# Key, query and output products of three cross-attention layers, each as two 64-column products, and the denominators scheduled one step later

## The chip, the core and the metric

The kernel runs on one core of a Trainium2 chip. The metric is the time of one execution on the device, in microseconds (us); lower is better. The engines of the core are named as the profile names them: PE (matrix products; PEld is its weight loading), DVE, ACT and POOL (element-wise work), SP (it issues nearly all DMA transfers here).

## The reference

Four cross-attention layers follow each other on x (2048 rows of 256 values), all with the same context of 1601 rows of 512 values. Layers 0, 2 and 3 are the **masked** ones: 16 heads of 64 values, and a bias on the logits of four token columns.

```python
q = x @ Wq                      # 256 -> 1024 = 16 heads x 64
k = ctx @ Wk; v = ctx @ Wv      # 512 -> 1024
logits = einsum('bhqd,bhkd->bhqk', q, k) * 64**-0.5 + col_bias   # col_bias: mask by token column
probs = softmax(logits, axis=-1)
out = einsum('bhqk,bhkd->bhqd', probs, v)
x = out.reshape(...) @ Wo + bo + x
```

Layer 1 is the **grouped** one: RMS norm of x, 16 query heads of 16 values over 4 key/value heads, softmax, output product, residual. Everything is float32.

## The kernel before

**Tiling.** A masked layer is done in 8 blocks of two heads (2 x 64 = 128 feature columns); a block has four units, one for each 512 query rows. The 1601 keys are 13 chunks (twelve of 128, one of 65), and a unit takes 13 steps, one per chunk, two steps at a time ("pair of steps"). The grouped layer has 4 blocks of four heads in a scheme of its own.

**A step of a masked unit.** `masked_scores` (L715) makes the transposed scores of both heads, 128 keys x 512 queries each, from two products with 64 contracted rows. ACT copies them out (L727) into one of 22 buffers `p`, and DVE keeps a running maximum (L732). When a unit's 13 steps are through, `maxima` transposes the maxima on PE (L775), DVE reduces them (L776), and two DMAs by way of DRAM (`cols`, then `spread`, L678 and L681) put them on all partitions; ACT copies that to PSUM (L801). 18 steps after its scores a chunk gets the subtraction (DVE, L806), the exponential (ACT, L811) and its share of the sum (POOL, L814 for the first chunk, L816 for the others), and two steps later the product with the values (PE, L851): two products of 128 contracted rows and 64 columns, one for each head, the first into partitions 0 to 63 of `po`, the second into 64 to 127.

**The pieces.** Between these steps PE gets "pieces" of other work:

- keys of the next block (`keys`, L461): for two chunks at a time, 128 weight columns, four products of 128 rows in a row, over 256 columns of context; the 13th chunk is alone, with 65 columns;
- values of the next block (`two_values`, L415): 128 context columns as weights, 128 columns of Wv moving;
- queries of the next unit (`queries`, L485): 128 weight columns, two products over 512 columns;
- the finish of a unit: `add_up` (L884) sums the denominators over partitions, in two products of 64 columns; ACT copies the result to `by` (L888), two small DMAs bring it to `dens` (L893); `denominators` takes the reciprocal (DVE, L901), sends it to DRAM (`cols`, L678) and fetches it back to all partitions of `by` (two DMAs, L681); `divide` multiplies on POOL (L920); `project` makes the output product (L930), 128 weight columns, two products over 512 columns, and adds to x (L937, L942).

**What sets the order.** PE, DVE and ACT keep the written order, held by dependencies without semaphores at the end of the function; POOL and SP keep theirs as queues. `finish` gives each piece of a masked unit's end a due step, counted from the step in which the unit's last values are made; `Pieces.own` takes what is due up to the later step of a pair. So a due step of +2 lies in the next pair in any case, and one of +3 in the next pair for a unit that ends in the first step of a pair, and one pair later for a unit that ends in the second. 13 is odd, so units of the two kinds alternate. Pieces due come first; keys and values of the next block fill up, at most one piece that shares `pm` to a pair; after a unit's last scores the pieces come ahead of the next scores. A unit of the last block of layers 0 and 2 has `at = 10`, other masked units `at = 12`; the last block of layer 3 has a list of its own.

**Tiling of a product.** PE can hold products of fewer rows or columns beside each other. The built program names for each product which division of the array it uses: the scores (L715) 64 rows x 128 columns, the values (L851) and `add_up` (L884) 128 x 64, and keys, values' projection, queries, output product and transposes the whole 128 x 128. A float32 product is two passes in the trace, so the four products of two steps' values show as x8.

Of the kernel before, what the change touches and what calls it, by code (L numbers as in the profile page):

```python
# [18 lines left out]
P = 128  # L19
# [7 lines left out]
Piece = namedtuple("Piece", "run cost shared", defaults=(True,))  # L27
# [7 lines left out]
def tile_cross_attention_stack(ctx: ExitStack, tc: tile.TileContext, t: dict, out: bass.AP):  # L35
# [33 lines left out]
    nc = tc.nc  # L69
# [5 lines left out]
    NCT = CT // P  # L75
# [179 lines left out]
    def width(c):  # L255

        return sum(m for _, m in TCH[c : c + 2])
# [146 lines left out]

    factors = dram.tile([NB, P, QT], FP, name="factors")

    def two_values(v, wv, c, ct):

        f = wv.shape[2]
        chunks = TCH[c : c + 2]  # L410
        m = chunks[0][1]
        pv = ps_m.tile([P, QB // P, P], FP, name="pm")
        for d, (_, md) in enumerate(chunks):
            for k in range(NCT):
                nc.tensor.matmul(  # L415
                    pv[:md, d, :f], ct(k)[:, d * P : d * P + md], wv[:, k, :],
                    start=(k == 0), stop=(k == NCT - 1),
                )
        nc.scalar.copy(v[:m, c : c + len(chunks), :], pv[:m, : len(chunks), :f])  # L419
# [5 lines left out]
    class Masked:  # L425
# [26 lines left out]
        def projections(self, u):  # L452


            def keys(c, ct):
                if u.kT is None:
                    u.kT = heads.tile([P, T], FP, name="kT")
                a, n = TCH[c][0], width(c)
                pk = ps_m.tile([P, QB], FP, name="pm")[:, :n]
                for k in range(NCT):  # L460
                    nc.tensor.matmul(pk, u.wk[:, k, :], ct(k), start=(k == 0), stop=(k == NCT - 1))  # L461
                nc.scalar.copy(u.kT[:, a : a + n], pk)

            def values(c, ct):
                if u.v is None:
                    u.v = heads.tile([P, NT, P], FP, name="v")
                two_values(u.v, u.wv, c, ct)

            return keys, values
# [7 lines left out]
        def query_pieces(self, unit):  # L477

            xt = unit.transposed_x()

            def queries():
                unit.q = heads.tile([P, QB], FP, name="q", bufs=3)
                pq = ps_m.tile([P, QB], FP, name="pm")
                for k in range(NC):
                    nc.tensor.matmul(  # L485
                        pq, unit.u.wq[:, k, :], xt[:, k, :], start=(k == 0), stop=(k == NC - 1)
                    )
                nc.scalar.mul(unit.q, pq, 64 ** -0.5)

            return [(11, Piece(queries, 2.0))]  # L490

    class Grouped:
# [44 lines left out]
        def projections(self, u):  # L537

            if u.n:
                return None  # L540

            def keys(c, ct):
                if self.ks is None:
                    self.ks = heads.tile([64, T], FP, name="ks", bufs=1)
                a, n = TCH[c][0], width(c)
                pk = ps_m.tile([P, QB], FP, name="pm")[:64, :n]
                for k in range(NCT):
                    nc.tensor.matmul(
                        pk, self.wk[:, k, :], ct(k), start=(k == 0), stop=(k == NCT - 1)
                    )  # L550
                nc.scalar.copy(self.ks[:, a : a + n], pk)

            def values(c, ct):
                if self.vs is None:
                    self.vs = heads.tile([P, NT, 64], FP, name="vs", bufs=1)
                two_values(self.vs, self.wv, c, ct)

            return keys, values
# [125 lines left out]
    class Unit:  # L684
# [239 lines left out]
        def project(self):  # L924

            k = 0
            for py in psum.heads(False)[0]:
                of = range(k, k + py.shape[1])
                for k in of:
                    nc.tensor.matmul(  # L930
                        py[:, k - of[0], :], self.u.wo[:, ts(k, P)], self.oT, start=True, stop=True
                    )
                k += 1
                if self.masked and self.u.n == self.layer.BLOCKS - 1 - (self.l == len(layers) - 1):
                    for j in of:
                        bo, to = bo_of[self.layer.l][:, j : j + 1], xs[:, self.b, j, :]
                        nc.vector.scalar_tensor_tensor(  # L937
                            to, py[:, j - of[0], :], bo, to, ALU.add, ALU.add
                        )
                else:  # L940
                    to = xs[:, self.b, of[0] : k, :]
                    nc.vector.tensor_tensor(to, py, to, ALU.add)  # L942
# [41 lines left out]
        def finish(self):  # L984

            if self.very_last:
                return [(0, Piece(lambda: self.quarters(of[len(units) - 2]), 2.0))]
            if self.final:

                at = 4 if self.b == NB - 2 else 2  # L990
                found = [
                    (at, Piece(self.add_up, 1.0)), (at + 2, Piece(self.denominators, 0.0)),
                    (at + 4, Piece(self.divide, 0.0)),
                ]
                if self.b < NB - 2:
                    found.append((10 - 2 * self.b, Piece(self.project_rows, 2.0, False)))
                return found
            if not self.masked:
                return [
                    (1, Piece(self.den_columns, 0.0)), (3, Piece(self.denominators, 0.0)),  # L1000
                    (6, Piece(self.divide, 0.0)), (8, Piece(self.project, 2.0, False)),
                ]

            at = 10 if self.u.n == self.layer.BLOCKS - 1 else 12
            return [
                (2, Piece(self.add_up, 1.0)), (4, Piece(self.denominators, 0.0)),
                (at - 4, Piece(self.divide, 0.0)), (at, Piece(self.project, 2.0, False)),
            ]

# [5 lines left out]
    for b in range(NB):  # L1015
        nc.scalar.dma_start(
            out=x_rows[b], in_=x[0, ts(b, QB), :].rearrange("(n p) c -> p n c", p=P)
# [377 lines left out]
```

## Time and profile before

| | |
|---|---|
| median of 3 runs | 4650.75 us (4649.49 to 4656.12) |
| the profiled execution | 4649.11 us, its span 4647.2 us |
| PE busy | 4529.5 us (97% of the span) |
| DVE, ACT, POOL busy | 3611.4, 3263.8, 2983.5 us (78%, 70%, 64%) |
| mean granted PE clock | 0.987 |
| products in the program | 12,524, in two passes each where they are float32 |

The span is the time from the first to the last instruction on the core. The busy time of an engine is the union of its instructions; for PE the ends of products are modelled, so the distances between the starts of consecutive groups say more than the busy share. In a timeline row the first number is the start in us from the span's start, the second how long the group lasted, and `x8` the number of passes in it.

### The profile page before, as it was taken

What the parts mean: (1) busy time and instruction counts of PE and PEld (TensorE: products, weight loads), DVE (VectorE), ACT (ScalarE), POOL (GpSimd) and SP (SyncE); (2) the same over time, 40 slices, a digit from 0 to 9 for tenths busy, and PEclk for the clock granted to TensorE, in tenths of its full rate; (3) what the DMA queues carried; (4) which work ended last, traced back from release to release, by engine and by line L of the source; (5) the groups of instructions that cost most, each with busy time, mean ns of one, the idle gap of its engine ahead of it and who ended that gap; (6) DMA issues with size and microseconds to landing.
All of it is one profiled execution on the core that took longest, in us unless ns stands there. A gap on an engine that the chain in (4) does not pass through costs nothing.

```text
span 4647.2 us, 64011 instructions
## 1 busy us (share of the span) xinstructions
PE 4529.5 (97%) x23563; PEld 1853.4 (40%) x23563; DVE 3611.4 (78%) x3672; ACT 3263.8 (70%) x4108; POOL 2983.5 (64%) x1436
## 2 busy tenths in 40 slices
PE   8999999999899999999999999999999999999998
PEld 5444434443333333343344444344444444344432
DVE  5888888888766666652678888888888888888887
ACT  5777777777645555555667777777777777777776
POOL 3888888888620000000578887888888888878887
PEclk9999999999989999998899999999999999999999
DMA  5333333233201100021233333233232323332311
GB/s 160 85 90 82 87 81 88 78 86 84 71 24 34 28 22 22 20 62 31 70 91 82 88 82 87 77 88 85 77 94 82 92 82 87 81 88 78 85 38 39
DMA packets 377252, 338.01 MB, mean 73 GB/s; under 512 B 143781, under 2 KB 332741, under 8 KB 376940
## 3 DMA queue, kind: packets, MB, share of 16 engines
q1 hardware_dynamic: 373670, 328.54, 26.2%
q8 instruction: 186, 3.05, 0.3%
q0 software_dynamic: 1152, 3.28, 0.2%
q10 hardware_dynamic: 2118, 2.10, 0.1%
q14 instruction: 126, 1.03, 0.1%
HBM read 318.49 MB, written 14.69 MB: 72 GB/s over the span
## 4 chain that ended last, share of the span: by engine, by line
PE 90%; DVE 4%; ACT 2%; POOL 1%; issue 1%; DMA 1%; SPq 0%; ACTq 0%; DVEq 0%; POOLq 0%
PE po L851 28%; PE s L715 23%; PE t L746 9%; PE pm L415 6%; PE pm L461 6%; PE pm L485 4%; PE s L930 4%; DVE top L732 3%; PE s L775 2%; PE pm L884 2%; ACT p L727 2%; POOL sums L816 1%; PE t L821 1%; PE s L821 1%; PE pm L597 1%
## 5 line engine op out<-in xcount | busy, mean ns | idle before, releaser
L816 POOL TENSOR_TENSOR sums<-sums,p 128x1024 f32<-128x1024 f32 x1145 | 2714.9, 2371 | 627.3 <-ACT p L811 555.1
L732 DVE TENSOR_TENSOR top<-s,top 128x1024 f32<-128x1024 f32 (+1 forms) x1056 | 1290.8, 1222 | 344.6 <-ACT p L727 288.8
L851 PE MATMUL po<-p,v 128*64 128x512 f32 (+3 forms) x8320 | 1500.9, 526 | 6.4 <-ACT p L811 3.7
L806 DVE TENSOR_TENSOR p<-p,b 128x1024 f32<-128x1024 f32 (+1 forms) x1248 | 1478.2, 1208 | 1.9 <-ACT b L801 1.7
L727 ACT COPY p<-s 128x1024 f32<-128x1024 f32 (+1 forms) x1248 | 1224.0, 1015 | 336.2 <-PE s L715 276.8
L715 PE MATMUL s<-q,kT 64*128 64x512 f32 (+1 forms) x4992 | 1295.9, 625 | 43.8 <-DVE top L732 39.8
L811 ACT ACTIVATE p<-p 128x1024 f32<-128x1024 f32 (+1 forms) x1248 | 1264.6, 1058 | 39.5 <-DVE p L806 39.1
L851 PEld LDWEIGHTS po<-p,v 128*64 128x64 f32 (+3 forms) x8320 | 367.2, 125 | 1128.3 <-issue 989.1
L715 PEld LDWEIGHTS s<-q,kT 64*128 64x128 f32 (+1 forms) x4992 | 403.9, 182 | 756.3 <-DVE top L732 383.2
L833 ACT ACTIVATE p<-t 128x512 f32<-128x512 f32 (+1 forms) x760 | 413.9, 594 | 296.8 <-PE t L821 256.4
L759 DVE TENSOR_REDUCE row_top<-t 128x1 f32<-128x512 f32 x700 | 451.3, 687 | 199.1 <-PE t L821 166.5
L920 POOL TENSOR_TENSOR by<-oT,by 128x512 f32<-128x512 f32 x111 | 141.1, 1271 | 708.5 <-DMA by<-cols 521.6
L821 PE MATMUL t<-q,kT 32*128 32x512 f32 (+1 forms) x1520 | 489.6, 644 | 0.0
L746 PE MATMUL t<-kT,q 32*128 32x512 f32 (+1 forms) x1880 | 482.7, 553 | 0.0
L415 PEld LDWEIGHTS pm<-wv,ct 128*128 128x128 f32 (+1 forms) x2600 | 302.4, 187 | 89.2 <-issue 67.1
L415 PE MATMUL pm<-wv,ct 128*128 128x128 f32 (+2 forms) x2600 | 326.9, 278 | 2.2 <-ACT v L419 0.9
L461 PE MATMUL pm<-ct,wk 128*128 128x256 f32 (+1 forms) x1344 | 309.2, 373 | 3.6 <-DMA ct<-ctxT 2.1
L461 PEld LDWEIGHTS pm<-ct,wk 128*128 128x128 f32 x1344 | 233.3, 191 | 119.1 <-issue 83.2
L730 DVE TENSOR_TENSOR top<-s,p 128x1024 f32<-128x1024 f32 x96 | 117.6, 1225 | 202.8 <-ACT p L727 202.7
L746 PEld LDWEIGHTS t<-kT,q 32*128 32x128 f32 x1880 | 182.8, 185 | 164.1 <-issue 97.4
L776 DVE TENSOR_REDUCE ntop<-s 128x8 f32<-128x1024 f32 x96 | 117.6, 1225 | 123.7 <-PE s L775 123.7
L930 PE MATMUL s<-by,wo 128*128 128x512 f32 x376 | 187.8, 622 | 12.6 <-issue 6.9
(173 smaller groups left out, 2085.8 us busy)
## 6 DMA issues: line engine op xcount, KB each, us to landing
ct<-ctxT SPq DMA_DIRECT2D x288, 512.0 KB
xT<-xT SPq DMA_DIRECT2D x100, 512.0 KB
spread<-cols SPq DMA_DIRECT2D x96, 512.0 KB
by<-cols SPq DMA_DIRECT2D x190, 128.0 KB
xT<-xs SPq DMA_DIRECT2D x16, 512.0 KB
ct<-ctxT SPq DMA_DIRECT2D x48, 130.0 KB
wk<-in_L_xattn_Wk_dram SPq DMA_DIRECT2D x24, 256.0 KB
wv<-in_L_xattn_Wv_dram SPq DMA_DIRECT2D x24, 256.0 KB
```

Source lines behind the costliest of these rows:

```text
L415: nc.tensor.matmul(pv[:md, d, :f], ct(k)[:, d * P : d * P + md], wv[:, k, :], start=(k == 0), stop=(k == NCT - 1),)
L461: nc.tensor.matmul(pk, u.wk[:, k, :], ct(k), start=(k == 0), stop=(k == NCT - 1))
L715: nc.tensor.matmul(s[:m, h, :], self.u.kT[r, a : a + m], self.q[r, :], start=True, stop=(a != TAIL),)
L727: nc.scalar.copy(p[:m], s[:m])
L732: nc.vector.tensor_tensor(self.top[:m], s[:m], self.top[:m], ALU.max)
L746: nc.tensor.matmul(s[:, at : at + n], self.q[r, ts(q, P)], self.u.kT[r, a : a + n], start=True, stop=True,)
L759: nc.vector.tensor_reduce(self.top[:, of, q, k : k + 1], s, AX.X, ALU.max)
L806: nc.vector.tensor_tensor(self.p[c][:m], self.p[c][:m], self.less[:m], ALU.add)
L811: nc.scalar.activation(p[:m], p[:m], AF.Exp)
L816: nc.gpsimd.tensor_tensor(self.sums[:m], self.sums[:m], p[:m], ALU.add)
L821: nc.tensor.matmul(s[:m], self.u.kT[r, a : a + m], self.q[r, :], start=True, stop=True)
L851: nc.tensor.matmul(to, v, p, start=(c == 0 and not part), stop=(c == NT - 1 and part != 0))
```

## The change

`halved` makes a product with 128 weight columns as two products of 64 columns, into partitions 0 to 63 and 64 to 127 of the same output, in the order in which the values' products of the two heads come. Keys, queries and the output product of the masked layers use it; the values' projection, the transposes and the grouped layer stay as they were. In the finish of a masked unit the due steps of `add_up` and `denominators` become `at - 9` and `at - 7`: 3 and 5 instead of 2 and 4 where `at` is 12, and 1 and 3 in the last block of layers 0 and 2, where it is 10. `divide` and `project` keep their due steps. Lines after the new function move down by 7.

```diff
+    def halved(out, cols, rows, **kwargs):
+        n = cols.shape[-1]
+        step = 64 if n == P else n
+        for at in range(0, n, step):
+            nc.tensor.matmul(out[at : at + step], cols[:, at : at + step], rows, **kwargs)
...
                 for k in range(NCT):
-                    nc.tensor.matmul(pk, u.wk[:, k, :], ct(k), start=(k == 0), stop=(k == NCT - 1))
+                    halved(pk, u.wk[:, k, :], ct(k), start=(k == 0), stop=(k == NCT - 1))
...
                 for k in range(NC):
-                    nc.tensor.matmul(
+                    halved(
                         pq, unit.u.wq[:, k, :], xt[:, k, :], start=(k == 0), stop=(k == NC - 1)
                     )
...
                 for k in of:
-                    nc.tensor.matmul(
+                    (halved if self.masked else nc.tensor.matmul)(
                         py[:, k - of[0], :], self.u.wo[:, ts(k, P)], self.oT, start=True, stop=True
                     )
...
             at = 10 if self.u.n == self.layer.BLOCKS - 1 else 12
             return [
-                (2, Piece(self.add_up, 1.0)), (4, Piece(self.denominators, 0.0)),
+                (at - 9, Piece(self.add_up, 1.0)), (at - 7, Piece(self.denominators, 0.0)),
                 (at - 4, Piece(self.divide, 0.0)), (at, Piece(self.project, 2.0, False)),
             ]
```

## The prediction, made before the changed kernel ran

> **What bounds the kernel.** I read the page first, then the masked stretch by itself, then PE's timeline there.
>
> ```profile
> span 4647.2 us, 64011 instructions
> PE 4529.5 (97%) x23563; PEld 1853.4 (40%) x23563; DVE 3611.4 (78%) x3672; ACT 3263.8 (70%) x4108; POOL 2983.5 (64%) x1436
> PE 90%; DVE 4%; ACT 2%; POOL 1%; issue 1%; DMA 1%; SPq 0%; ACTq 0%; DVEq 0%; POOLq 0%
> ```
>
> PE is busy all along, and 90% of the chain that ended last is PE's. The stretch from 2400 to 4400 us holds masked layers alone; the first line gives its busy times, the second is the longest of PE's own waits in it.
>
> ```profile
> 2400.00:4400.00 2000.00, 1975.36 (x8841) 823.07 (x8840) 1681.17 (x1497) 1528.81 (x1785) 1635.20 (x746) 1.00 0.32 85
> PE s L715 <- DVE top L732: 18.9, 50, 0.8
> ```
>
> PE (1975 of 2000) is the bound; DVE (1681), POOL (1635) and ACT (1529) have a sixth or more to spare. A unit takes some 37.5 us, and PE waits about 0.4 us in it. So what the PE stream loses in length is what the time can lose.
>
> What does the stream consist of? The groups' starts in PE's timeline tell. Durations overlap, so I take the distance from one start to the next.
>
> ```profile
> 1005.54 1.94 PE L851 MATMUL po<-p,v 128*64 128x512 f32 x8
> 1007.40 1.98 PE L485 MATMUL pm<-xT,wq 128*128 128x512 f32 x4
> 1009.23 1.11 PE L775 MATMUL s<-ident,top 128*128 128x128 f32 x8
> 1010.18 1.95 PE L415 MATMUL pm<-wv,ct 128*128 128x128 f32 x16
> 1012.06 1.99 PE L715 MATMUL s<-q,kT 64*128 64x512 f32 x8
> ...
> 1019.63 2.05 PE L415 MATMUL pm<-wv,ct 128*128 128x128 f32 x16
> 1021.61 1.99 PE L715 MATMUL s<-q,kT 64*128 64x512 f32 x8
> 1023.53 1.94 PE L851 MATMUL po<-p,v 128*64 128x512 f32 x8
> 1025.39 1.98 PE L930 MATMUL s<-by,wo 128*128 128x512 f32 x4
> 1027.21 1.95 PE L415 MATMUL pm<-wv,ct 128*128 128x128 f32 x16
> 1029.09 1.08 PE L851 MATMUL po<-p,v 65*64 65x512 f32 x4
> ```
>
> And one place where two groups of the tiling 128 x 64 meet (the grouped layer's keys, 64 weight columns, 65 moving columns):
>
> ```profile
> 1150.53 1.94 PE L851 MATMUL po<-p,v 128*64 128x512 f32 x8
> 1152.30 0.63 PE L548 MATMUL pm<-ct,wk 128*64 128x65 f32 x8
> 1152.86 1.13 PE L715 MATMUL s<-q,kT 64*128 64x512 f32 x4
> ```
>
> Three readings. (a) **A change of tiling costs about 0.20 us when it leads into 128 x 128.** L415 behind another 128 x 128 group (1010.18, 1027.21) takes 1.88 us, behind L851 (1019.63) 1.98: 0.10 for a first weight load that nothing hides. And a group that is followed by another tiling is longer by 0.09: L851 takes 1.86 ahead of L485 or L930, and 1.77 ahead of L548 in its own tiling. Where L930 is followed by L415 in the same tiling, its 1.82 holds the first term alone. (b) **Two halves beside each other cost no more than one whole.** L851's 8 passes of 64 columns, two products at a time, take 1.77 us, entry included, for the work that L930's 4 passes of 128 columns do in 1.82. (c) With 65 moving columns a pass is bound by loading its weights: L548 needs 0.56 us for 8 passes with 64 columns of weights. The masked keys' 65-column group with 128 columns of weights, eight passes too (L461, starting at 1002.37; the next group at 1003.40), needs 1.03.
>
> **The change, part by part.**
>
> *Fewer changes of tiling.* Pieces usually stand between L851 (128 x 64) and L715 (64 x 128). A halved piece has L851's tiling, so the change ahead of it goes and the one behind it stays. Not all gain: queries are often followed by the transposes L775, and the output product by L415, and those then pay the entry that the piece paid before. Counted over PE's instruction lists of the two built programs, entries into 128 x 128 go from 433 to 240; all other kinds stay within 2 (128 x 64: 707 to 708, 64 x 128: 638 in both). 193 x 0.20 = **-39 us**.
>
> *The 65-column keys.* There is one such group in each of 24 blocks: 1.03 - 0.56 = 0.47, less some 0.05 of entry that the first term holds already, 24 x 0.42 = **-10 us**. This takes the two halves' weight loads to run beside each other, as (b) shows for 512 columns. From the other side, if they load one after the other, nothing is won here: 0.
>
> *More instructions.* 672 key, 192 query and 184 output products are doubled: 1048 more. By (b) they cost 0, taking the halves as L851's. One thing no row shows: L851's two halves stream different columns of `p`, the new ones stream the same rows twice. Bounds: 0, or the whole of the pieces once more if the array can't do this side by side. That is 576 key products of 0.43 us (two passes of 256 columns, half of L485's passes), 96 of 0.23, 376 of 0.86: 593 us. I take 0, the nearest row.
>
> The Trainium skill speaks against this part: TensorEngine Tiling (Array Packing), section Performance Considerations (Instruction Overhead), gives each matmul about 60 cycles of overhead and says not to take the tiling factor from a dimension that is already small; its section on when to tile wants 64 columns or fewer, and here there are 128. By that rule the 1048 products, two passes each, would add 2096 x 60 cycles, at the 2.4 GHz of TensorE: Matmul & The Clock Gate (its table of specs) an estimate of 52 us, and the sum would be near zero. The rows of (b) show no such overhead for a second half.
>
> *Denominators later.* With `at` = 12, only units that end in the second step of a pair move: two units in each of 21 blocks, 42 in all. In such a unit (last values copied at 2936.57) `add_up` stands at 2936.7 now, behind the output product, and moves two pairs on; a piece of values or keys takes its place, so PE's work stays the same. Behind it the reciprocal moves from 2948.35 to behind DVE's subtraction of 2952.01, about 2953.2, into the 0.34 us in which DVE waits ahead of L776: no cost. SP then issues the write of the reciprocals at about 2953.6, passing the fetch of the next x, and the two fetches of `by` behind a context slice, just ahead of `spread`. POOL and SP now:
>
> ```profile
> 2948.57 0.36 SPq L678 DMA_DIRECT2D cols<-rden  x1
> 2951.51 1.35 SPq L681 DMA_DIRECT2D by<-cols  x2
> ...
> 2958.21 0.34 SPq L681 DMA_DIRECT2D spread<-cols  x1
> ```
>
> ```profile
> 2944.46 12.14 POOL L816 TENSOR_TENSOR sums<-sums,p 128x1024 f32<-128x1024 f32 x5
> 2956.57 1.27 POOL L920 TENSOR_TENSOR by<-oT,by 128x512 f32<-128x512 f32 x1
> 2959.72 4.83 POOL L816 TENSOR_TENSOR sums<-sums,p 128x1024 f32<-128x1024 f32 x2 [1.89 <-ACT p L811]
> ```
>
> From the write to the first fetch it takes 3.0 us, from that to a divide that waited 3.6 to 5.7 (mostly 3.8 to 4.9) in the units of the other kind. So `by` is there at 2953.6 + 3.1 + 4.4 = 2961.1, and **POOL, free at 2956.6, waits some 4.5 us in the divide**. Queued behind it are the sums of the next unit: L816 starts at 2962.4 instead of 2959.7, 2.7 us late, and stays late for five chunks. Who waits for those? ACT's copy L727, 22 steps after a chunk's scores, needs the buffer back: after these sums it now starts 3.8, 2.3, 7.3, 5.8 and 6.2 us after the sum's end. So one copy (2966.8) comes 0.4 us late, where PE has an output product and keys to do before the next scores at 2973.1 and those scores' buffer would be free 2.6 us early: 0 on PE. The next `add_up`, at 2980.8, follows sums done at 2972.9: covered too. `spread` is issued when its own write has landed, as now (2958.2); its 512 KB may come up to 1 us later behind the 256 KB of `by`. ACT, which waits 0.39 us for it at 2963.47, then waits longer, under the same two pieces: 0 to 0.4 us on PE, 0 to 17 us over 42 units. I take 0, since the pieces cover it. With `at` = 10 units move one pair forward or not at all: no cost.
>
> **Sum.** -39 - 10 = -49 us of PE's stream. PE waits 24.6 us in the 2000 already, mostly for DVE at the start of a unit; some of a gain just ahead of such a wait is given back. DVE idles before those waits too, so they follow PE; I take 10% off, by choice: **-44 us**. The profiled execution (4649.1) would become 4605; the median shown is 1.6 above it, so 4650.75 - 44 = **4607 us**.
>
> **Rivals.**
>
> *Half is given back (4611 to 4641).* DVE is at 84% over the stretch, but two scores tiles are all that PE has ahead. If DVE's maxima keep their times at each unit's start, only about half of the -49 stays: about -25, 4626 us. For it: 50 waits for DVE, one a unit. Against: DVE is idle shortly before them.
>
> *No change (within 9 us).* The halves cost what is saved, 49 us over 1048 products, some 47 ns each. Against it: (b).
>
> *Slower: the divide's wait grows.* Up to a lag of the sums of 2.3 + 2.6 = 4.9 us nothing reaches PE; I expect 2.7. Past that each us costs 42 us. If the fetch of `by` behind a 512 KB slice lands not 4.4 but 8.5 us after its issue, the lag is 6.8, the loss 42 x 1.9 = 80, and the time 4650.75 - 44 + 80 = 4687 us; it outweighs the gain from about 7.7 us. For it: the divide's wait is new and on a queue that is 82% busy. Against: no divide that waited in this stretch shows more than 5.7.
>
> *Slower: the halves don't run side by side*, +593 less the -39 of the changes: about 5205 us. It would decide at once; the values and `add_up` argue against it.
>
> **How the numbers follow.** Forecast (4595 to 4611) 63%; half given back 22%; no change 6%; slower by the divide 6%; halves in series 3%. The range 4595 to 4638 takes the first two (85%). The bound for a change that a measurement of this kernel can tell is 0.2%, 9 us: faster 0.85, same 0.06, slower 0.09.
>
> **What would show it.** Right: L485's group behind L851 with x8 and 1.81 us to a following L715 (1.91 with both changes of tiling now), L851 ahead of it 1.77; the 65-column keys about 0.56; POOL's divide waiting for `by` in every second unit, 4 to 5 us, and PE's waits no longer than now. Wrong: a halved group of over 2 us, or PE waiting for ACT's copies or DVE where it didn't.

## The result, and the profile after

| | before | after |
|---|---|---|
| median | 4651.29 us, 4 runs (4649.49 to 4656.12) | 4693.76 us, 4 runs (4690.64 to 4697.03) |
| ratio, 95% interval | | 1.0085 [1.0073, 1.0097] |
| span of the profiled execution | 4647.2 us | 4688.8 us |
| products in the program | 12,524 | 13,572 |
| entries into the 128 x 128 tiling | 433 | 240 |

The change makes the kernel **slower by about 40 us**; the forecast was 44 us faster. All halved products have line 412, that of the product in `halved`. The page of the changed kernel, its span, busy times and chain by engine:

```profile
span 4688.8 us, 68217 instructions
PE 4501.4 (96%) x25659; PEld 1780.6 (38%) x25659; DVE 3615.3 (77%) x3672; ACT 3266.3 (70%) x4108; POOL 2982.6 (64%) x1436
PE 76%; DVE 10%; issue 5%; ACT 3%; DMA 2%; POOL 2%; another core or an unknown queue 0%; SPq 0%; ACTq 0%; DVEq 0%; POOLq 0%
```

PE's busy time fell by 28 us, as a saving in its stream would have it, but the span grew. PE's share of the chain went from 90% to 76%, and DVE's from 4% to 10%: the end is no longer set by PE alone. The stretch from 2400 to 4400 us (stretch, its length, then PE, PEld, DVE, ACT and POOL busy, with the number of instructions) says the same; behind the busy times stand the granted clock, the DMA share and GB/s:

```profile
2400.00:4400.00 2000.00, 1938.99 (x9886) 773.97 (x9884) 1658.10 (x1475) 1508.17 (x1759) 1611.84 (x736) 1.00 0.32 84
```

All engines are less busy than before at the same granted clock of 1.00: they wait more, for each other or for transfers. **The halves themselves are as forecast.** From PE's timeline:

```profile
3004.83 1.94 PE L858 MATMUL po<-p,v 128*64 128x512 f32 x8
3006.60 1.89 PE L412 MATMUL pm<-xT,wq 128*64 128x512 f32 x8
3008.41 1.08 PE L722 MATMUL s<-q,kT 64*65 64x512 f32 x4
...
3032.07 0.64 PE L412 MATMUL pm<-ct,wk 128*64 128x65 f32 x16
3032.64 2.31 PE L722 MATMUL s<-q,kT 64*128 64x512 f32 x8
```

From start to start, the values ahead of a halved group take 1.77 us, the halved queries 1.81, the 65-column keys 0.57; the three numbers given were 1.77, 1.81 and about 0.56. So the loss is in the waits. PE's and ACT's waits in the stretch (who waits for whom: us in total, times, longest):

```profile
PE s L412 <- issue: 31.5, 21, 2.0
PE s L722 <- DVE top L739: 18.9, 51, 0.6
```

```profile
ACT b L808 <- DMA spread<-cols: 48.6, 23, 4.1
ACT p L734 <- POOL sums L823: 38.9, 43, 1.4
```

In the kernel before, the same two waits were

```profile
PE s L930 <- issue: 4.3, 6, 1.4
ACT b L801 <- DMA spread<-cols: 10.0, 14, 1.6
```

PE's wait for DVE ahead of the scores is 18.9 us, as before. New is the wait of the output product (`s` at L412): 31.5 us in 21 places instead of 4.3 in 6, and another 6.6 us in 6 places that the profile puts down to POOL's sums (0.7 in one before). ACT's wait for `spread` grew from 10.0 us in 14 places to 48.6 in 23; its wait for POOL's sums came to 0.8 us before. POOL now waits some 196 us in the divide, against about 24.

Where does it come from? Units end at two kinds of places, and only those that end in the second step of a pair moved. Taking the copies of `oT` (one a unit) between units 52 and 92, a unit takes 37.58 us before and 37.99 after; the interval behind a unit that didn't move is 37.80 (38.00 before), behind one that moved 38.18 (37.17). All of the loss lies with the kind that moved. One of them in the timeline of the changed kernel, SP's queue first, then lines picked from POOL, ACT, PE and DVE; a bracket holds the engine's idle time just before and what ended it. The unit's last values were copied at 2956.2:

```profile
2972.72 0.37 SPq L685 DMA_DIRECT2D cols<-rden  x1
2974.12 0.36 SPq L685 DMA_DIRECT2D cols<-ntop  x1
2974.75 0.55 SPq L264 DMA_DIRECT2D ct<-ctxT  x1
2978.68 1.12 SPq L688 DMA_DIRECT2D by<-cols  x2
2979.86 0.58 SPq L688 DMA_DIRECT2D spread<-cols  x1
...
2983.72 1.27 POOL L927 TENSOR_TENSOR by<-oT,by 128x512 f32<-128x512 f32 x1 [7.64 <-DMA spread<-cols]
2984.70 1.02 ACT L808 COPY b<-spread 128x1024 f32<-128x1024 f32 x1 [2.16 <-DMA spread<-cols]
2984.95 12.12 POOL L823 TENSOR_TENSOR sums<-sums,p 128x1024 f32<-128x1024 f32 x5
2986.01 1.94 PE L858 MATMUL po<-p,v 128*64 128x512 f32 x8
2987.34 1.01 ACT L734 COPY p<-s 128x1024 f32<-128x1024 f32 x1 [0.38 <-POOL sums L823]
2988.39 1.23 DVE L739 TENSOR_TENSOR top<-s,top 128x1024 f32<-128x1024 f32 x1 [1.35 <-ACT p L734]
2989.71 1.94 PE L412 MATMUL s<-by,wo 128*64 128x512 f32 x8 [1.76 <-issue]
```

The write of the reciprocals (L685, `rden`) stands 1.4 us ahead of that of the maxima (`ntop`). The fetch of `by` is issued 6.0 us after its write, `spread` behind it, 5.7 us after its own. ACT, which runs in its written order, stands 2.16 us before L808, and 0.38 us more, for POOL's sums, before its copy L734. That copy of the scores out of PSUM comes late, so DVE's maximum over that tile (L739, done at 2989.62) is late, and PE's output product, which needs a scores tile to write to, starts at 2989.71 instead of 2987.78 (1.77 after L858): 1.93 us late. The same place before, where the timeline has

```profile
2963.47 1.02 ACT L801 COPY b<-spread 128x1024 f32<-128x1024 f32 x1 [0.39 <-DMA spread<-cols]
...
2966.59 1.94 PE L851 MATMUL po<-p,v 128*64 128x512 f32 x8
2966.95 2.56 DVE L732 TENSOR_TENSOR top<-s,top 128x1024 f32<-128x1024 f32 x2 [0.38 <-ACT p L727]
2968.46 1.98 PE L930 MATMUL s<-by,wo 128*128 128x512 f32 x4
```

shows how little room there was: the first of the two maxima is done at about 2968.2, and the output product starts at 2968.46. With 0.3 us to spare, the lateness reaches PE almost in full: ACT's wait for `spread` is 1.77 us longer than before and its wait for POOL 0.38, together 2.15, and PE is 1.93 late. So in this unit both the late `spread` and POOL have a part, the first the larger one.

A correction to the description of the kernel: PE, DVE and ACT keep the written order, but POOL and SP do not; the build's scheduler orders their queues and they then run in that order. A due step moves their instructions only by way of what these wait for.

### The profile page after: what moved, and what is told of

Same layout as the page of the kernel before. It is cut to its first block, busy times and chain, and to the rows that moved or that the text cites. A ratio compares the mean times of both kernels' runs of the same rounds, so it can differ in the third digit from the quotient of the medians.

```text
span 4688.8 us, 68217 instructions
## 1 busy us (share of the span) xinstructions
PE 4501.4 (96%) x25659; PEld 1780.6 (38%) x25659; DVE 3615.3 (77%) x3672; ACT 3266.3 (70%) x4108; POOL 2982.6 (64%) x1436
## 4 chain that ended last, share of the span: by engine, by line
PE 76%; DVE 10%; issue 5%; ACT 3%; DMA 2%; POOL 2%; another core or an unknown queue 0%; SPq 0%; ACTq 0%; DVEq 0%; POOLq 0%
PE po L858 23%; PE s L722 19%; PE t L753 9%; PE pm L412 7%; PE pm L422 6%; DVE top L739 6%; PE s L412 3%; DVE p L813 3%; ACT p L734 2%; PE s L782 2%; POOL sums L823 2%; PE pm L891 2%; PE t L828 1%; DMA cols<-rden 1%; PE s L828 1%
## 5 line engine op out<-in xcount | busy, mean ns | idle before, releaser
L739 DVE TENSOR_TENSOR top<-s,top 128x1024 f32<-128x1024 f32 (+1 forms) x1056 | 1290.3, 1222 | 330.3 <-ACT p L734 275.0
L858 PE MATMUL po<-p,v 128*64 128x512 f32 (+3 forms) x8320 | 1497.5, 524 | 9.7 <-ACT p L818 6.7
L734 ACT COPY p<-s 128x1024 f32<-128x1024 f32 (+1 forms) x1248 | 1226.3, 1014 | 373.1 <-PE s L722 256.9
L858 PEld LDWEIGHTS po<-p,v 128*64 128x64 f32 (+3 forms) x8320 | 367.9, 125 | 1127.0 <-issue 919.9
L422 PEld LDWEIGHTS pm<-wv,ct 128*128 128x128 f32 (+1 forms) x2600 | 301.2, 188 | 98.5 <-issue 43.4
L422 PE MATMUL pm<-wv,ct 128*128 128x128 f32 (+2 forms) x2600 | 329.7, 279 | 2.8 <-ACT v L426 1.4
L412 PE MATMUL pm<-ct,wk 128*64 128x256 f32 (+1 forms) x2688 | 296.3, 363 | 7.4 <-issue 7.1
L412 PE MATMUL s<-by,wo 128*64 128x512 f32 x728 | 179.6, 613 | 62.9 <-issue 52.4
L412 PEld LDWEIGHTS pm<-ct,wk 128*64 128x64 f32 x2688 | 182.8, 139 | 146.9 <-issue 70.9
```

Of the source, the lines that this page charges most:

```text
L412: nc.tensor.matmul(out[at : at + step], cols[:, at : at + step], rows, **kwargs)
L422: nc.tensor.matmul(pv[:md, d, :f], ct(k)[:, d * P : d * P + md], wv[:, k, :], start=(k == 0), stop=(k == NCT - 1),)
L734: nc.scalar.copy(p[:m], s[:m])
L739: nc.vector.tensor_tensor(self.top[:m], s[:m], self.top[:m], ALU.max)
L858: nc.tensor.matmul(to, v, p, start=(c == 0 and not part), stop=(c == NT - 1 and part != 0))
```

## The experiments

Twelve runs; each ratio is against the kernel before on the same chip.

| run | median us | ratio, 95% interval |
|---|---|---|
| `halves_only` | 4615.66 | 0.9923 [0.9906, 0.994] |
| `due_only` | 4732.26 | 1.0167 [1.0144, 1.0191] |
| `divide_later` | 4703.09 | 1.0114 [1.0096, 1.0133] |
| `spread_first` | 4688.6 | 1.0082 [1.0064, 1.01] |
| `hop` | 4672.01 | 1.0047 [1.0031, 1.0063] |
| `spread_ahead` | 4661.31 | 1.0016 [1.0006, 1.0027] |
| `write_behind` | 4623.25 | 0.9936 [0.992, 0.9952] |
| `fetch_by_act` | 4765.02 | 1.0249 [1.023, 1.0269] |
| `keys_only` | 4640.07 | 0.9973 [0.9961, 0.9985] |
| `queries_only` | 4642.43 | 0.9978 [0.9969, 0.9988] |
| `output_only` | 4642.9 | 0.9975 [0.9967, 0.9984] |
| `values_too` | 4602.38 | 0.9898 [0.9878, 0.9917] |

**The theories.** A: the halves gain, and the move of the denominators costs more. B, the rival: the doubled products cost, and the move is free. Within A: A1, POOL's longer wait in the divide holds its sums back, and with them ACT's copies; A2, the late `spread` holds ACT.

### Which part loses: `halves_only` and `due_only`

`halves_only` is the change with the old due steps; `due_only` is the kernel before with the new ones.

```diff
-                (at - 9, Piece(self.add_up, 1.0)), (at - 7, Piece(self.denominators, 0.0)),
+                (2, Piece(self.add_up, 1.0)), (4, Piece(self.denominators, 0.0)),
```

> The changed kernel with the due steps of before (add_up 2, denominators 4). Theory A: the halves are what was worked out (entries into 128 x 128 fall from 433 to 241, 65-column keys shorter) and the move of the denominators took it back: 4600 to 4618 us. Theory B: the doubled instructions themselves cost more than they save: 4680 to 4700 us, about the changed kernel's time.

> The kernel before with the new due steps alone, products whole. Its own order removes 40 entries into 128 x 128 and 42 into 128 x 64, about 14 us. Theory A: the move costs about 2 us in each of 42 units, less the 14: 4705 to 4735 us. Theory B: the move is harmless: 4635 to 4650 us.

The halves alone gain 0.77%, about 36 us; the move alone costs 1.67%, 78 us. Both lie in the range of theory A. The sum, 42 us, is close to the 40 of the whole change. Theory B falls: 1048 more products, and the time goes down.

### POOL's wait or the late spread: `divide_later`, `spread_first`, `hop`

`divide_later`, the changed kernel with the divide two steps later:

```diff
-                (at - 4, Piece(self.divide, 0.0)), (at, Piece(self.project, 2.0, False)),
+                (at - 2, Piece(self.divide, 0.0)), (at, Piece(self.project, 2.0, False)),
```

> The changed kernel with the divide of masked units due two steps later (at - 2), output product where it was. If POOL's wait in the divide, and the sums queued behind it that hold ACT's copies back, are the cause (A1): most of the loss goes, 4610 to 4640 us, and ACT's copies wait for POOL no longer. If the late spread that holds ACT is the cause (A2): 4670 to 4695 us, unchanged but for a little.

It tells nothing of the theories. The scheduler put POOL's and SP's queues in the same order as without the edit, and the waits are those of the changed kernel (ACT's for `spread` 46.5 us).

`spread_first`, the changed kernel with the fetches of `by` in a piece of their own, due five steps ahead of the output product, in the moved units:

```diff
+            self.fetch_later = at == 12 and self.b % 2 == 1
+            fetch = [(at - 5, Piece(lambda: self.fetch(), 0.0))] if self.fetch_later else []
+            return fetch + [
```

> The changed kernel, but in the 42 moved units the two fetches of by are issued behind spread instead of ahead of it; the divide stays where it is. A2 (late spread): most of the loss goes, 4610 to 4650 us. A1 (POOL's wait in the divide): the divide waits about 1 us longer, so 4690 to 4730 us, while ACT's waits for spread fall from 49 us to about 10 in the stretch from 2400 to 4400 us.

The edit did not do what was meant: the scheduler still left one fetch of `by` ahead of `spread`, so `spread` came no earlier; but it put the divide two sums later on POOL. POOL's waits in the stretch:

```profile
POOL sums L829 <- ACT p L824: 274.0, 106, 4.0
POOL by L934 <- DMA by<-cols: 35.6, 22, 3.4
```

The divide's waits have fallen from some 196 us to about 62, ACT's copies no longer wait for POOL's sums, ACT's wait for `spread` is 49.3 us, and the time is within 5 us of the changed kernel, inside the intervals. So **A1 falls as the main cause**: with POOL's hold on ACT taken away, nearly the whole loss is still there. A small part may be POOL's: behind a unit of the kind that moved, the interval between units 52 and 92 is 37.93 us here, against 38.18 in the changed kernel and 36.71 in `halves_only`.

`hop` does the opposite. It is `halves_only` with one more copy of 4 KB in DRAM ahead of `spread` in the 42 units, and nothing moved:

```diff
+        if hop:
+            again = dram.tile([4, P, QT], FP, name="again", bufs=4)[:n]
+            nc.sync.dma_start(out=again, in_=rows)
+            rows = again
```

> The halves with the due steps of before, and in the 42 units that the change would move spread gets one more small transfer ahead of it (cols to a copy of cols, 4 KB, and spread is fetched from the copy), so that spread alone comes some 2.5 us later; POOL and the denominators stay as they were. A2 (a late spread is what costs): 42 x 2 to 2.5 us on top of 4616, 4690 to 4725 us. A1 (POOL's wait in the divide is what costs): 4612 to 4630 us.

```profile
ACT b L813 <- DMA spread<-again: 47.6, 22, 3.1
```

ACT's wait in the stretch is that of the changed kernel, POOL's divide waits no longer than before, and against `halves_only` the ratio rises by 0.0124, about 58 us. That is below the 4690 to 4725 that A2 expected and far above the 4612 to 4630 of A1. ACT's copy L808 follows the write of the maxima by 10.4 us in the units of this kind, as in the changed kernel (8.9 in `halves_only`). So a `spread` that reaches ACT as late as in the changed kernel, with nothing else moved, costs three quarters of the move's price. The interval behind a unit of this kind is 37.93 us, the same as in `spread_first`, the other kernel in which `spread` is late and POOL doesn't hold ACT. Between units 52 and 92 the late `spread` thus makes 37.93 - 36.71 = 1.22 us of the 1.47 that the change loses there, and 0.25 us, some 10 us over 42 units, go with POOL. These intervals come from one profiled execution of each kernel; the ratios alone, good to 0.0012 to 0.0018 each (6 to 8 us), can't tell the 10 us from nothing.

### What makes spread late: `spread_ahead`, `write_behind`, `fetch_by_act`

`spread_ahead` is `spread_first` with the fetches of `by` bound behind `spread` on SP's queue; `write_behind` binds the write of the reciprocals behind it as well:

```diff
+        def behind():
+            if later and spread_at:
+                ins = nc.cur_bb.bb.instructions[-1]
+                tc.add_manual_dep(ins, spread_at[-1].name, order_only, reason="behind spread")
...
                 nc.sync.dma_start(out=rows.rearrange("h p q -> p h q"), in_=cols)
+            behind()
             for tile_, heads_ in to:
...
                 nc.sync.dma_start(out=tile_, in_=src.to_broadcast(tile_.shape))
+                behind()
```

The code is that of `write_behind`, where the write stands in the later piece with the fetches; `spread_ahead` binds the two fetches alone and leaves the write where the change has it.

> The changed kernel, with both fetches of by in the 42 moved units held behind spread on SP's queue by a dependency; the build then puts the divide two sums later on POOL. A2: spread is issued some 3.3 us after its write again, ACT's wait for it shrinks to that of before, 4610 to 4640 us. If something else of the move costs (a third cause, neither POOL nor spread): 4670 to 4695 us.

> The changed kernel, but on SP's queue of the 42 moved units the write of the reciprocals goes behind spread as well, with the two fetches of by behind it; so nothing of the reciprocals stands between the write of the maxima and spread any more. The divide then stands two sums later on POOL. If the late spread is the cause (its wait for by's fetches, and its own write landing late behind the write of the reciprocals), ACT's wait for spread falls back to some 10 us in the stretch from 2400 to 4400 (1.6 us each or less), and the time to that of the halves alone and below the 4661 of spread_ahead: 4612 to 4635. If what is left there comes from something else in the move (the later sums, the piece that takes the place of add_up, POOL's order), ACT's wait may fall but the time stays at 4650 or above.

`spread_ahead` lies between its two expectations, `write_behind` in the first of its own. The time falls in two steps: 0.0069, 32 us, for the fetches, and another 0.0080, 37 us, for the write. In the moved units `spread_first` has the divide two sums later on POOL as well, and from there the first step is 0.0066, 31 us: the steps aren't POOL's. With both, the ratio is 0.9936, that of `halves_only` within the intervals: **the whole price of the move is gone, though `add_up` and the reciprocal still stand where the change put them.** SP's queue in a moved unit of `write_behind`, and its ACT's wait in the stretch:

```profile
2938.32 0.34 SPq L728 DMA_DIRECT2D xT<-xT  x1
2940.73 0.37 SPq L694 DMA_DIRECT2D cols<-ntop  x1
2941.36 0.88 SPq L264 DMA_DIRECT2D ct<-ctxT  x1
2943.01 0.33 SPq L698 DMA_DIRECT2D spread<-cols  x1
2943.39 0.43 SPq L694 DMA_DIRECT2D cols<-rden  x1
```

```profile
ACT b L825 <- DMA spread<-cols: 0.8, 2, 0.5
```

The columns below are means over the units that end in the second step of a pair, 26 or 27 in the stretch, two or three of them unmoved, from the timeline: from the write of the maxima to the issue of `spread`, from the write to ACT's copy L808, ACT's idle time ahead of the copy, and the price against `halves_only` by the ratios, for each of 42 units:

| | write to `spread` | write to ACT's copy | ACT idle | price a unit |
|---|---|---|---|---|
| before | 3.72 | 8.64 | 0.36 | |
| `halves_only` | 4.20 | 8.87 | 0.49 | 0 |
| the change | 4.86 | 10.43 | 2.05 | 1.8 |
| `spread_first` | 4.69 | 10.50 | 2.12 | 1.8 |
| `hop` | 6.52 | 10.39 | 2.01 | 1.4 |
| `spread_ahead` | 4.39 | 9.97 | 1.60 | 1.0 |
| `write_behind` | 2.69 | 8.37 | none | 0.1 |

The price goes with the time at which ACT gets `spread`. In `write_behind` POOL still waits 56.5 us for `by`, more than in the kernel before (14.7), and it costs nothing that shows; but with the divide two sums later ACT waits for POOL less than 3 us there, so this run says little of A1 by itself.

Why ACT gets it late is only partly told. From `halves_only` to the change the issue of `spread` moves by 0.66 us and ACT's copy by 1.56; the other 0.90 lie between the issue and the copy (5.57 us against 4.67), where `by`'s 256 KB are fetched just ahead of `spread`. In `spread_ahead`, where they are fetched just behind it, that part is still 5.58 us, and the issue, 4.39 us after the write, is hardly later than the 4.20 of `halves_only`. `write_behind` takes the write of the reciprocals from ahead of `spread` and also moves `by`'s fetches from 0.5 to 5.4 us behind its issue (means over the moved units). That the three transfers of the reciprocals make `spread` late is shown; how much each does by holding the issue, and how much by delaying the 512 KB behind the issue, is not.

`fetch_by_act` issues the fetches of `by` from ACT's queue instead:

```diff
+            queue = nc.scalar if later else nc.sync
...
+                queue.dma_start(out=tile_, in_=src.to_broadcast(tile_.shape))
```

> The changed kernel, with the fetches of by in the 42 moved units issued from ACT's queue one pair later, so that SP's queue has nothing between the write of the maxima and spread but a context slice; the divide stays at its place on POOL, so POOL waits some 8 us in it. A2 alone: 4610 to 4640 us. A1 and A2 together: POOL's lateness still holds ACT's copies, 4650 to 4680 us.

A miss, and the slowest of all. ACT's wait for `spread` is down to 7.2 us, but now ACT stands ahead of its own issue until the reciprocals' write has landed: ahead of its copies of values and keys it stands 114 us in 17 places of the stretch, up to 8.7 us at a time, and PE waits 32.9 us for ACT's copy of the scores. A wait was moved from a queue that issues transfers to an engine that everyone needs.

### Where the halves gain: `keys_only`, `queries_only`, `output_only`, `values_too`

Three kernels halve one kind of product each, with the denominators where they were. `values_too` is `halves_only` with the values' projection (L422) halved as well:

```diff
-                nc.tensor.matmul(
+                halved(
                     pv[:md, d, :f], ct(k)[:, d * P : d * P + md], wv[:, k, :],
```

> Halves for the masked keys alone, with the denominators where they were before. By the stream: entries into 128 x 128 fall from 433 to 356 (77 x 0.20 = -15), entries into 128 x 64 rise from 707 to 767 (60 of some 0.15 = +9), the 65-column groups give -10: together about -16, 4634. If the halves of the keys cost their weight loads one after the other (0 for the 65-column groups), about -6, 4644. If the gain of halves_only comes from one kind of product alone, that kind shows all 35.

> Halves for the masked queries alone, with the denominators where they were before. Entries into 128 x 128 fall from 433 to 386 (47 x 0.20 = -9), into 128 x 64 rise by 4: about -9, 4641. If PE's waits for DVE at a unit's start give it back, within 3 us of the kernel before.

> Halves for the masked output projection alone, with the denominators where they were before. Entries into 128 x 128 fall from 433 to 386 and into 128 x 64 from 707 to 667 (47 x 0.20 + 40 x 0.15 = -15): about 4635. If the gain is given back just ahead of PE's waits for DVE at a unit's start, which come right behind this product, within 5 us of the kernel before.

> The halves with the due steps of before, and the values' projection of masked layers (and of chunks of 128 context columns in general) halved as well. Entries into 128 x 128 go from 241 to 172, into 128 x 64 from 710 to 745: 69 x 0.20 - 35 x 0.15 = 8.5 us of PE's stream. If most of it stays: 4604 to 4612 us. If the doubled products of 128 moving columns are bound by their weight loads or their issue: above 4620 us.

By the ratios keys bring 13 us, queries 10 and the output product 12, each good to 4 to 6 us, together the 35 of `halves_only`; no kind gives its share back entirely. The values' projection adds some 11 us more (the intervals of the two ratios still overlap a little), with 241 entries into 128 x 128 become 172 (69 x 0.20 = 14, with 35 more entries into 128 x 64 against it). `values_too`, 1.02% faster than the kernel before, is the fastest version here.

## Why the prediction was wrong

**The step that failed is "Denominators later".** It put the move at no cost; measured, it costs 78 us alone and about 75 on top of the halves, 1.8 us in each of 42 units. Three of its statements fell.

- "`spread` is issued when its own write has landed, as now (2958.2)". It was seen that SP issues the write and the two fetches just ahead of it, but only the 256 KB of `by` were counted as a delay, up to 1 us. In the unit shown `spread` is issued 5.7 us after its write instead of 3.4, behind two fetches that wait for the other write; on average ACT gets it 10.4 us after the write instead of 8.6, and its idle time grows by 1.7 us, where 1 was the most. Taking the fetches, then the write, out of the way of `spread` gives 32 us and 37 us back (`spread_ahead`, `write_behind`).
- "ACT ... then waits longer, under the same two pieces: 0 to 0.4 us on PE, 0 to 17 us over 42 units. I take 0, since the pieces cover it." One of the two pieces is the output product, and its group in the profile reads `s<-by,wo`: it writes to a scores tile, the very thing that ACT's copy and DVE's maximum have to free. It was no cover but the first to wait, with some 0.3 us to spare. The range was too low: in the unit shown PE is 1.93 us late, and the price over the 42 units is 1.8 us each.
- "From the write to the first fetch it takes 3.0 us", so that `by` is there at +7.5. In the moved units the fetch comes 4.43 us after the write on average, 6.0 in the one shown, and POOL waits up to 8.4 us where 4.5 were expected. This was worked out with most care, and it mattered least: some 10 us, by the intervals above.

**The rival on the other side** gave 4687 us, near the 4694 measured, by POOL's lag. That lag nearly came: in the unit shown POOL is free at 2976.1 and the next sums start at 2984.95, 8.9 us later instead of 3.2, a lag of 5.7 us against the 4.9 from which the rival counts a loss. But `spread_first` takes POOL's hold on ACT away and nearly all of the loss stays. Its number is near by chance.

**The sum of the stream held in its mechanism and was too large.** 192 of the 193 entries go with the halves alone, and the three group lengths are those forecast; -49 less 10% was put down, and 36 came. Over the 96 masked units 49 us are 0.51 a unit. Between units 52 and 92 a unit fell from 37.58 to 37.25 us, by 0.33. PE's waits that the profile lists in the stretch grew from 24.5 to 27.9 us, 0.06 a unit, about the 10% taken off; so some 0.39 us a unit were saved, and it is the terms of the sum that were too large, by about a quarter. Which of them isn't shown: `keys_only`, `queries_only` and `output_only` lie within 4 us of their own sums, inside their intervals. The first rival, half given back because DVE keeps its times, isn't what happened: PE's wait for DVE ahead of the scores grew by 3.5 us in the stretch, from 18.9 to 22.4. A part may lie at the start: in the one profiled execution of each kernel, the last values of the first unit are copied at 127.1 us before, and at 132 to 136 in all the others, `due_only` with its whole products too. With one profile each that can be chance, and it stays open.

**That the second half costs nothing** held as far as the runs can tell: the halved groups have the forecast lengths, and if all that the stream's sum missed in the 96 units were put on the 1048 products, it would be some 11 ns each. TensorEngine Tiling (Array Packing) in the Trainium skill, Performance Considerations (Instruction Overhead), with its 60 cycles for each matmul, would have left the halves' sum near zero by the estimate in the prediction; `halves_only` and `values_too` decide against that for halves that run side by side. The same page, Tiling Modes (Key Properties), says that a change of tiling mode drains the engine, which agrees with the 0.09 us that a group is longer ahead of one; it gives no price.

## What to carry to other kernels

Before a wait is called covered, look at what the covering work writes to: a piece that needs the resource that the late engine frees is not cover. When a step moves, read the queue that issues its transfers in order, with the waits of each entry: a fetch that waits for its own write holds everything behind it, and moving a second small write from just ahead of a critical one to behind that one's fetch, its own fetches with it, brought 37 us here. Where small products stand between groups of a 64-column tiling, splitting them to stay in that tiling is worth a try even if nothing in them is small.

## What the runs showed of the hardware

How long a write of 4 KB to DRAM takes (1024 values, in 256 pieces of four) differed with what was issued ahead of it on the queue. From the write of the maxima to the issue of the fetch that waits for it, on average, it took 4.39 us with the write of the reciprocals some 1.4 us ahead (`spread_ahead`) and 2.69 with that write moved behind (`write_behind`). But it also took 4.20 in `halves_only`, where the nearest small write ahead stands about 6 us earlier and `by`'s 256 KB are fetched 2.8 us ahead. So the small write isn't shown to be the reason by itself. DMA: Bandwidth & Descriptors in the Trainium skill, Queues, rings and completion order, says that the signal of a transfer's end lands only after every earlier write of the same DMA engine; that agrees in direction with both, but no run here separates it from the time the queue takes to work through what stands ahead.

In `write_behind` the fetch of `by` is issued 5.0 us on average after the reciprocals' write where that stands right behind the 512 KB of `spread`, and 3.1 in the other units. A small write is late behind a large fetch as well; here the order decided which transfer had to bear it.
